# A selective-scan network: sums of product pairs on GpSimd, PSUM banks of two pools in turn, and the last stage in reversed column order

## Chip, cores, metric

The kernel runs on one core of one Trainium2 chip. The metric is the device time of one execution in microseconds. The times before are the median of three runs; the profile comes from one profiled execution of its own.

## What is computed

The input x has the shape (8, 64, 64, 64): eight images of 64 channels, 64 x 64 pixels, in float32. Four layers follow one another:

```
x = layer0(x)   # attention over all 4096 pixels, then 3x3 depthwise, 1x1, and x is added
x = layer1(x)   # layer norm; two blocks of 8x8 window attention and an MLP (the second shifted)
x = layer2(x)   # nine taps with dynamic filters, leaky relu, a 9-tap row convolution, plus x
x = layer3(x)   # selective scan in four directions, gating, then pooled depthwise branches
```

The part that the change touches most is the scan of layer 3. For each image, direction k, channel (128 of them) and state n (16 of them), over the 4096 pixels in the order of the direction:

```
h = h * exp(dt_t[..., None] * A) + dt_t[..., None] * B_t[:, :, None, :] * u_t[..., None]
y_t = einsum('bkcn,bkn->bkc', h, C_t)
```

The four directions' y are summed, normalised over the channels, gated with silu(z), and projected. The rest of layer 3 (`back` below) adds that to its input, normalises over the channels again, and forms four depthwise branches, three of them after max pooling by 2, 4 and 8, which are aggregated, passed through gelu, multiplied and added.

## The kernel before, in words

Images are handled in four pairs; the 128 partitions are two images of 64 channels, or the 128 channels of one image's scan. A pair has three parts, in class `_Direct`:

- `front(p)` (line 1225): layer 0 to layer 2, then `scan_sources` (line 1549), which leaves the scan's inputs and the gate z in DRAM.
- `scans(p, ...)` (line 1614): 64 units (2 images x 4 directions x 8 blocks of 512 columns), each of 8 steps of two states: 512 steps.
- `back(p)` (line 1748): what follows the scan. A first loop over 8 blocks of 512 columns (lines 1754 to 1774) reads ys of both images, normalises, gates, projects and adds, and normalises over the channels into the padded tile F. The pooled branches follow (1777 to 1802), then a second loop over the 8 blocks (1803 to 1826), with the depthwise taps of the full-size branch and the output.

`tile_kernel` (line 1831) runs front(0) alone, then for each pair p the scans with back(p-1) and front(p+1) beside them, and at the end back(3) alone. `front` and `back` are generators that yield costs. `scans` draws from them so that their summed cost keeps pace with the steps: `while done < cost * (i + 1) / (n - LEAD)`, with LEAD = 24, so the work beside should be out of the way 24 steps before the end. The cost of a back is put at a quarter of a front's; by its own yields it comes to 264 units against 2,016, so that it runs out earlier: in phases 1 and 2 some 67 steps before the end, in the last phase, which has back(2) alone beside it, at about the middle. After that `next(beside, cost)` returns the whole cost.

A step (`step`, line 1682) handles states n and n+1. Two steps ahead, GpSimd has formed v = B * du for both (1680, 128 x 1024). ScalarE writes da = exp(A dt) into a PSUM bank (1700), VectorE scans (1703), ScalarE copies the last column into the carries (1711). Then the products with C: `rp` is `i % 2 or u["image"] >= B - 2` (1689). Where it is 0 (even steps of images 0 to 5), GpSimd does both states in one instruction of 1024 columns (1714). Where it is set, GpSimd does one state (1716) and VectorE the other (1717). One step later `sums` (1719) adds the two products to y with two matmuls against the identity (1730); each matmul shows as two records in the profile. After eight steps y goes to Y or, for the last direction, to ys in DRAM (1739 to 1745). The directions run in the order 1, 3, 0, 2; direction 2 goes through the column blocks from 7 down to 0.

Each fetch of B and C (1675, 512 KB each) is issued on SP's queue, as are the scan's inputs (1652, 1668), ys (1745) and the loads of back (1756, 1761, 1762).

[...] Pool `ps_scan` holds three of tag "da" (da, and pdd and pbc of `inputs`, 1654 and 1663) and one for y; pool `ps_front` holds three of tag "f", which `bank()` (1178) gives to front and back, and one for `total()`. The order of instructions on each engine isn't the program's: the framework's scheduler arranges it when the kernel is built, with program order as the priority.

Of the kernel before, what the change touches and what calls it, by code (L numbers as in the profile page):

```python
# [9 lines left out]
F32 = mybir.dt.float32  # L10
AF = mybir.ActivationFunctionType
ALU = mybir.AluOpType
# [3 lines left out]
B, C, HH, WW = 8, 64, 64, 64  # L16
L = HH * WW
P = 128
CH = 512
NCH = L // CH  # L20
# [3 lines left out]
DI, NST, RNK, KDIR = 128, 16, 4, 4  # L24
TD = 512
# [1122 lines left out]
class _Direct:  # L1148
# [8 lines left out]
    def __init__(self, net, ctx):  # L1157
        self.net, self.tc, self.nc, self.w = net, net.tc, net.nc, net.w
        tc = self.tc
        self.dram = ctx.enter_context(tc.tile_pool(name="mem", bufs=2, space=bass.MemoryType.DRAM))  # L1160
        one = ctx.enter_context(tc.tile_pool(name="scan1", bufs=1))
        self.Y = one.tile([P, L], F32, name="Y", tag="Y")
        self.carries = one.tile([P, NST], F32, name="carry", tag="carry")
        self.sw = ctx.enter_context(tc.tile_pool(name="scan", bufs=2))
        self.slabs = ctx.enter_context(tc.tile_pool(name="slabs", bufs=3))
        self.ps = ctx.enter_context(tc.tile_pool(name="ps_scan", bufs=3, space=PSUM))
        self.pf = ctx.enter_context(tc.tile_pool(name="ps_front", bufs=3, space=PSUM))
        self.kept = {}

    def padded(self, name):  # L1170
        t = self.slabs.tile([P, SLAB], F32, name=name, tag="slab").rearrange("p (h w) -> p h w", w=66)
# [3 lines left out]
    def flat(self, name):  # L1175
        return self.slabs.tile([P, SLAB], F32, name=name, tag="slab")[:, 0:L]

    def bank(self, name, shape=(P, CH)):
        return self.pf.tile(list(shape), F32, name=name, tag="f")

    def total(self, name, shape=(P, CH)):
        return self.pf.tile(list(shape), F32, name=name, tag="acc", bufs=1)
# [431 lines left out]
    def scans(self, p, beside, cost):  # L1614

        self.units = []
        for im in range(2):
            out = self.memory("ys")  # L1620
            self.kept["y", 2 * p + im] = out
            for nth, k in enumerate((1, 3, 0, 2)):
                order = range(NTD) if k < 2 else range(NTD - 1, -1, -1)
                self.units += [dict(image=2 * p + im, k=k, c=c, at=at, nth=nth, out=out) for at, c in enumerate(order)]
        self.inputs(self.units[0])
        n = 8 * len(self.units)
        steps = [{} for _ in range(n)]
        done = 0
        for i in range(-3, n):
            if i + 3 < n:  # L1630
                self.fetch(i + 3, steps[i + 3], 0)
            if 0 <= i + 2 < n:
                self.fetch(i + 2, steps[i + 2], 1)
                self.products(i + 2, steps[i + 2])
            if i >= 0:
                self.step(i, steps[i])
                if i:
                    self.sums(i - 1, steps[i - 1], steps[i]["w"])
                while done < cost * (i + 1) / (n - LEAD):
                    done += next(beside, cost)  # L1640
            if i % 8 == 1 and i // 8 + 1 < len(self.units):
                self.inputs(self.units[i // 8 + 1])
        self.sums(n - 1, steps[n - 1])
        self.run(beside)
# [37 lines left out]
    def step(self, i, st):  # L1682

        nc, w, net = self.nc, self.w, self.net
        wk, ps = self.sw, self.ps
        u = self.units[i // 8]
        k, c, at, CC, v = u["k"], u["c"], u["at"], st["C"], st["v"]

        n0, rp = 2 * (i % 8), i % 2 or u["image"] >= B - 2
        rev = k >= 2  # L1690

        def along(t):
            return t[:, ::-1] if rev else t

        h = wk.tile([P, 2 - i % 2, TD], F32, name="hd", tag=f"h{i % 2}", bufs=1)
        hs = []
        for j in range(2):
            n = n0 + j
            da = ps.tile([P, TD], F32, name="dad", tag="da")
            nc.scalar.activation(da, u["du"][:, 0], AF.Exp, scale=net.As[:, k, n : n + 1])  # L1700
            first = 0.0 if at == 0 else self.carries[:, n : n + 1]
            to = da if rp and j else h[:, j]
            nc.vector.tensor_tensor_scan(along(to), along(da), along(v[:, j]), first, ALU.mult, ALU.add)  # L1703
            hs.append(to)
            if at < NTD - 1 and (rp or j):
                ends = h[:, :, 0] if rev else h[:, :, TD - 1]
                cs = self.carries[:, n0 : n0 + 2]
                if rp:
                    ends = to[:, 0:1] if rev else to[:, TD - 1 : TD]
                    cs = self.carries[:, n : n + 1]  # L1710
                nc.scalar.activation(cs, ends, AF.Copy)  # L1711

        if rp == 0:
            st["w"] = nc.gpsimd.tensor_tensor(v, h, CC, ALU.mult)  # L1714
        else:
            st["w"] = nc.gpsimd.tensor_tensor(v[:, 0], h[:, 0], CC[:, 0], ALU.mult)  # L1716
            nc.vector.tensor_tensor(v[:, 1], hs[1], CC[:, 1], ALU.mult)  # L1717

    def sums(self, i, st, after=None):

        nc, w, net = self.nc, self.w, self.net
        wk, ps = self.sw, self.ps
        u = self.units[i // 8]
        k, c = u["k"], u["c"]
        if i % 8 == 0:
            u["y"] = ps.tile([P, TD], F32, name="yd", tag="y", bufs=1)
        y = u["y"]
        for j in range(2):
            n = 2 * (i % 8) + j
            m = nc.tensor.matmul(y, lhsT=w["ident"], rhs=st["v"][:, j], start=(n == 0), stop=(n == NST - 1))  # L1730
            if after is not None and j == 0:
                net.behind(m, after)
        if i % 8 < 7:
            return

        yd = net.part(self.Y, k, c)
        yp = y.rearrange("p (a b) -> p a b", b=64)
        if u["nth"] == 0:
            nc.vector.scalar_tensor_tensor(yd, self.img(u["x"]), net.dsum, yp, ALU.mult, ALU.add)
        elif u["nth"] < 3:  # L1740
            nc.vector.tensor_tensor(yd, yd, yp, ALU.add)  # L1741
        else:
            o = wk.tile([P, TD], F32, name="yo", tag="yo", bufs=1)
            nc.vector.tensor_tensor(self.img(o), yd, yp, ALU.add)
            nc.sync.dma_start(u["out"][:, c * TD : (c + 1) * TD], o)


    def back(self, p):
        nc, tc, w, net, half = self.nc, self.tc, self.w, self.net, self.HALF
# [1 line left out]
        X = self.flat("X3")  # L1751
        F = self.padded("F")
        with tc.tile_pool(name="w4", bufs=2) as wk:
            for c in range(NCH):
                cols = slice(c * CH, (c + 1) * CH)
                nc.sync.dma_start(X[:, cols], self.kept["x", p][:, cols])
                po = self.bank("po3")
                for im in range(2):
                    y = wk.tile([P, CH], F32, name="yb", tag="yb")
                    z = wk.tile([P, CH], F32, name="zb", tag="zb")  # L1760
                    nc.sync.dma_start(y, self.kept["y", 2 * p + im][:, cols])
                    nc.sync.dma_start(z, self.kept[2 * p + im][2][:, cols])
                    pc, sd = self.normed(wk, lambda pc: [(pc, y)], w["cen128"], w["avg128"], net.eps[:, 0:1])
                    u = wk.tile([P, CH], F32, name="u", tag="u")
                    nc.vector.scalar_tensor_tensor(u, pc, w["on_g"], sd, ALU.mult, ALU.mult)  # L1765
                    nc.vector.scalar_tensor_tensor(u, u, w["on_b"], z, ALU.add, ALU.mult)  # L1766
                    nc.tensor.matmul(po[half[im]], lhsT=w["opT"], rhs=u, start=True, stop=True)  # L1767
                    yield 6
                nc.vector.scalar_tensor_tensor(X[:, cols], po, w["outproj_b"], X[:, cols], ALU.add, ALU.add)  # L1769
                pc, sd = self.normed(wk, lambda pc: [(pc, X[:, cols])], w["cen64"], w["avg64"], net.eps[:, 1:2])  # L1770
                d = self.rows(F, c)
                nc.vector.scalar_tensor_tensor(d, self.img(pc), w["cn_g"], self.img(sd), ALU.mult, ALU.mult)
                nc.scalar.activation(d, d, AF.Identity, bias=w["cn_b"])
                yield 6
# [56 lines left out]
def tile_kernel(ctx: ExitStack, tc: tile.TileContext, x: bass.AP, packs, layout, out: bass.AP):  # L1831
    net = _Net(ctx, tc, x, packs, layout, out)
    with ExitStack() as path:
        net.open(path, True)
        d = _Direct(net, path)
        net.log_exp()
        front = d.run(d.front(0))
        back = 0.25 * front
        for p in range(B // 2):
            works, cost = [], 0  # L1840
            if p:
                works.append(d.back(p - 1))
                cost += back
            if p + 1 < B // 2:
                works.append(d.front(p + 1))
                cost += front
            d.scans(p, d.chain(*works), cost)
        d.run(d.back(B // 2 - 1))
# [31 lines left out]
```

## Time and profile before

| | us |
|---|---|
| median of 3 runs | 14083.28 (14071.26 to 14084.42) |
| profiled execution, its own time | 14074.21 |
| its span in the profile | 14072.3 |
| PE busy | 11340.1 (81%) |
| VectorE (DVE) busy | 8432.1 (60%) |
| ScalarE (ACT) busy | 7036.3 (50%) |
| GpSimd (POOL) busy | 8173.2 (58%) |
| mean granted PE clock | 0.865 |

The profile lists the busy time of each engine, the span in 40 slices of 352 us, and the costliest groups of instructions by line: how many, how long in all and each, and how long the engine sat idle just before them and for whom. Times are counted from the start of the span. A PE record's end is modelled, since matmuls are pipelined, so start-to-start distances say more than durations there. PEld are weight loads, which overlap with matmuls.

### The profile page before, as it was taken

Reading aid. Unit: us, or ns where it says so; the run is one execution under the profiler, and the core shown is the slowest. Engines: PE = TensorE matmul, PEld = TensorE weight load, DVE = VectorE, ACT = ScalarE, POOL = GpSimd, SP = SyncE. Lnnn points to the kernel's source line nnn. Section 1 sums busy time; section 2 is a strip of 40 time slices with the busy share of each in tenths; the row PEclk is TensorE's granted clock in tenths of the full one; section 3 lists DMA queues with packets and bytes.
Section 4 is the critical chain, followed back from the end, with each engine's and each line's share of the span. In section 5 each row is a group of like instructions: output and inputs, shape, how many; then the busy total and the mean of one; then the engine's idle time right before and its main releaser. Section 6 shows DMA issues by size and latency. Waiting matters only on the chain. (4 is left out here: it accounts for less than half of the span.)

```text
span 14072.3 us, 141532 instructions
## 1 busy us (share of the span) xinstructions
PE 11340.1 (81%) x46358; PEld 4189.8 (30%) x46358; DVE 8432.1 (60%) x9763; ACT 7036.3 (50%) x15453; POOL 8173.2 (58%) x4111
## 2 busy tenths in 40 slices
PE   9888879979889668998889666998988866666665
PEld 2244222224433222223433222222443222222221
DVE  0222254467776875347675767336666677998884
ACT  5533145555553645555562644555554454454442
POOL 0000035677776765456674685456666678879991
PEclk9866679989889889998898788999888878988996
DMA  0000034456555764345553675345554577878882
GB/s 17 1 1 1 5 136 153 161 187 211 195 196 181 241 206 156 127 147 181 175 197 133 225 247 180 128 144 175 170 173 168 181 244 256 276 241 291 294 291 70
DMA packets 705498, 2379.22 MB, mean 169 GB/s; under 512 B 81060, under 2 KB 81188, under 8 KB 703980
## 3 DMA queue, kind: packets, MB, share of 16 engines
q1 hardware_dynamic: 681024, 2315.57, 48.5%
q10 hardware_dynamic: 23724, 54.50, 1.0%
q8 instruction: 367, 6.01, 0.2%
q14 instruction: 383, 3.14, 0.1%
HBM read 2269.08 MB, written 100.66 MB: 168 GB/s over the span
## 5 line engine op out<-in xcount | busy, mean ns | idle before, releaser
L1680 POOL TENSOR_TENSOR vd<-B,du 128x1024 f32<-128x1024 f32 x2048 | 4842.5, 2369 | 3955.8 <-DVE xacc L1217 1888.8
L1730 PE MATMUL yd<-vd,pack 128*128 128x512 f32 x8192 | 4577.0, 686 | 1175.1 <-POOL vd L1714 419.8
L1703 DVE TENSOR_TENSOR_SCAN hd<-dad,carry,vd 128x512 f32<-128x512 f32 x2464 | 3092.6, 1270 | 1081.7 <-ACT dad L1700 681.2
L1700 ACT ACTIVATE dad<-du,As 128x512 f32<-128x512 f32 x4096 | 2711.7, 679 | 985.0 <-DVE hd L1703 728.8
L1730 PEld LDWEIGHTS yd<-vd,pack 128*128 128x128 f32 x8192 | 1592.5, 212 | 3853.7 <-issue 1753.0
L1714 POOL TENSOR_TENSOR vd<-hd,C 128x1024 f32<-128x1024 f32 x768 | 1810.9, 2358 | 1365.4 <-DVE hd L1703 694.1
L1716 POOL TENSOR_TENSOR vd<-hd,C 128x512 f32<-128x512 f32 x1280 | 1634.9, 1278 | 271.7 <-DVE hd L1703 244.6
L1272 ACT ACTIVATE e<-s 128x512 f32<-128x512 f32 x2048 | 1199.2, 591 | 1030.0 <-PE s L1266 1028.1
L1703 DVE TENSOR_TENSOR_SCAN dad<-dad,carry,vd 128x512 f32<-128x512 f32 x1120 | 1426.0, 1273 | 62.7 <-ACT dad L1700 62.5
L1266 PE MATMUL s<-X 64*128 64x512 f32 x4096 | 1350.1, 646 | 114.1 <-ACT e L1272 113.8
L1258 PE MATMUL po<-e,VT 128*64 128x512 f32 x4096 | 1145.1, 629 | 17.0 <-ACT e L1272 17.0
L1711 ACT ACTIVATE carry<-hd 128x1 f32<-128x1 f32 (+1 forms) x1792 | 357.1, 201 | 1172.7 <-DVE hd L1703 1161.9
L1717 DVE TENSOR_TENSOR vd<-dad,C 128x512 f32<-128x512 f32 x1280 | 858.7, 671 | 82.1 <-ACT carry L1711 74.8
L1266 PEld LDWEIGHTS s<-X 64*128 64x128 f32 x4096 | 365.3, 186 | 1065.4 <-issue 820.8
L1420 PEld LDWEIGHTS w_av<-vals,w_e 64*64 64x64 f32 x16384 | 612.7, 159 | 178.0 <-ACT w_e L1410 69.9
L1420 PE MATMUL w_av<-vals,w_e 64*64 64x9 f32 x16384 | 638.5, 216 | 23.6 <-ACT w_e L1410 23.5
L1703 DVE TENSOR_TENSOR_SCAN hd<-dad,vd 128x512 f32<-128x512 f32 x352 | 420.2, 1210 | 203.0 <-ACT dad L1700 92.0
L1741 DVE TENSOR_TENSOR Y<-Y,yd 128x512 f32<-128x512 f32 x128 | 124.6, 973 | 656.0 <-PE yd L1730 655.7
L1410 ACT ACTIVATE w_e<-w_e 128x512 f32<-128x512 f32 x512 | 310.4, 627 | 382.2 <-DVE w_e L1405 254.9
L1655 PE MATMUL pdd<-xs,xdt 128*128 128x512 f32 x512 | 323.4, 718 | 204.3 <-DVE hd L1703 96.7
L1711 ACT ACTIVATE carry<-dad 128x1 f32<-128x1 f32 x1120 | 189.9, 170 | 589.1 <-DVE dad L1703 587.0
L1405 DVE TENSOR_TENSOR w_e<-w_s,bias 128x512 f32<-128x512 f32 x512 | 328.5, 682 | 248.4 <-PE w_s L1393 248.1
(247 smaller groups left out, 11078.1 us busy)
## 6 DMA issues: line engine op xcount, KB each, us to landing
B<-rows SPq DMA_DIRECT2D x2048, 512.0 KB, 5.0
C<-rows SPq DMA_DIRECT2D x2048, 512.0 KB, 4.5
xs<-xt SPq DMA_DIRECT2D x128, 256.0 KB, 2.9
xs<-xc SPq DMA_DIRECT2D x128, 256.0 KB, 3.1
xc<-xcv ACTq DMA_DIRECT2D x64, 256.0 KB, 4.3
zs<-z ACTq DMA_DIRECT2D x64, 256.0 KB, 3.9
xt<-XT ACTq DMA_DIRECT2D x32, 512.0 KB, 7.5
rows<-bc SPq DMA_DIRECT2D x256, 64.0 KB, 1.9
```

Of the source, the lines that this page charges most:

```text
L1258: nc.tensor.matmul(po[half[im]], lhsT=VT[:, t, half[im]], rhs=es[im], start=(t == 0), stop=(t == 31))
L1266: nc.tensor.matmul(ss[im], lhsT=at(half[im], t), rhs=X[half[im], jc * CH : (jc + 1) * CH], start=True, stop=True)
L1272: nc.scalar.activation(e, ss[im], AF.Exp, scale=C**-0.5, accum_out=parts[:, im, t, jc : jc + 1])
L1420: nc.tensor.matmul(self.av[half[im], x % 4 + j, h, :], lhsT=es[h // 4][half[im], j, h % 4, :], rhs=V[half[im], x + j, h, :], start=True, s ...
L1680: self.nc.gpsimd.tensor_tensor(v, st["B"], dx.to_broadcast([P, 2, TD]), ALU.mult)
L1700: nc.scalar.activation(da, u["du"][:, 0], AF.Exp, scale=net.As[:, k, n : n + 1])
L1703: nc.vector.tensor_tensor_scan(along(to), along(da), along(v[:, j]), first, ALU.mult, ALU.add)
L1711: nc.scalar.activation(cs, ends, AF.Copy)
L1714: st["w"] = nc.gpsimd.tensor_tensor(v, h, CC, ALU.mult)
L1716: st["w"] = nc.gpsimd.tensor_tensor(v[:, 0], h[:, 0], CC[:, 0], ALU.mult)
L1717: nc.vector.tensor_tensor(v[:, 1], hs[1], CC[:, 1], ALU.mult)
L1730: m = nc.tensor.matmul(y, lhsT=w["ident"], rhs=st["v"][:, j], start=(n == 0), stop=(n == NST - 1))
```

## The change

Four edits. `bank()` gets a second tag and a counter `turn`: while it is not negative, successive tiles are taken in turn from tag "f" of one pool and tag "da" of the other, so from six banks in place of three. It is not negative while front(0) runs alone, and in the last phase from the moment when the work beside is exhausted, to the end of the kernel; `da` of a step is then drawn in the same way. On even steps of images 0 to 5 GpSimd adds the second product to the first after it has formed both, and `sums` issues one matmul for that step in place of two. And the first loop of `back` goes through the column blocks from 7 to 0, in every pair.

```diff
@@ __init__
         self.kept = {}
+        self.turn = -1
@@ bank
-    def bank(self, name, shape=(P, CH)):
-        return self.pf.tile(list(shape), F32, name=name, tag="f")
+    def bank(self, name, shape=(P, CH), ours="f"):
+        if self.turn >= 0:
+            self.turn += 1
+            ours = ("f", "da")[self.turn % 2]
+        return (self.pf if ours == "f" else self.ps).tile(list(shape), F32, name=name, tag=ours)
@@ scans
                     self.sums(i - 1, steps[i - 1], steps[i]["w"])
+                if p == B // 2 - 1 and done >= cost:
+                    self.turn = max(self.turn, 0)
@@ step
-            da = ps.tile([P, TD], F32, name="dad", tag="da")
+            da = self.bank("dad", (P, TD), "da")
@@ step
         if rp == 0:
-            st["w"] = nc.gpsimd.tensor_tensor(v, h, CC, ALU.mult)
+            nc.gpsimd.tensor_tensor(v, h, CC, ALU.mult)
+            st["w"] = nc.gpsimd.tensor_tensor(v[:, 0], v[:, 0], v[:, 1], ALU.add)
+            st["n"] = 1
@@ sums
-        for j in range(2):
-            n = 2 * (i % 8) + j
-            m = nc.tensor.matmul(y, lhsT=w["ident"], rhs=st["v"][:, j], start=(n == 0), stop=(n == NST - 1))
+        n = st.get("n", 2)
+        for j in range(n):
+            m = nc.tensor.matmul(
+                y, lhsT=w["ident"], rhs=st["v"][:, j], start=(i % 8 + j == 0), stop=(i % 8 == 7 and j == n - 1)
+            )
@@ back, first loop
-            for c in range(NCH):
+            for c in reversed(range(NCH)):
@@ tile_kernel
+        d.turn = 0
         front = d.run(d.front(0))
+        d.turn = -1
```

## The prediction

> **What bounds the kernel now.** I read the page first, then one table of busy times cut at the stages of the work that runs beside the scans (I found the cuts from the first and last instruction of each stage's lines), then the costliest groups, the waits inside a stage, and the timeline of the two stretches where one side runs alone.
>
> ```profile
> span 14072.3 us, 141532 instructions
> ...
> PE 9888879979889668998889666998988866666665
> ...
> POOL 0000035677776765456674685456666678879991
> ...
> PEclk9866679989889889998898788999888878988996
> ```
> Three regimes. GpSimd (POOL) does nothing for the first 1,890 us: the front of pair 0 runs alone. Then come three scan phases beside other work (POOL's first product of each: 1905, 4990, 8348 us), a fourth from 11700 us that ends at 13785 us, and 287 us of the last back alone.
>
> The stage table, columns: stretch, length, busy us (and count) of PE, PE weight loads, DVE, ACT, POOL, then clock and DMA.
> ```profile
> 2003.00:2955.00 952.00, 911.31 (x2664) 251.82 (x2664) 412.17 (x388) 554.97 (x1567) 570.91 (x278) 0.98 0.48 162
> ...
> 3136.00:4130.00 994.00, 881.17 (x7042) 424.96 (x7041) 726.04 (x888) 600.01 (x1154) 755.69 (x368) 0.90 0.60 204
> ...
> 6285.00:6447.00 162.00, 105.36 (x278) 42.13 (x277) 153.76 (x175) 68.84 (x135) 132.48 (x64) 0.81 0.59 208
> 6450.00:7352.00 902.00, 804.81 (x6869) 396.00 (x6867) 610.94 (x786) 537.08 (x1015) 598.57 (x291) 0.89 0.53 180
> 7355.00:7742.00 387.00, 356.94 (x718) 130.34 (x718) 212.08 (x254) 113.18 (x235) 197.68 (x96) 0.88 0.41 138
> ...
> 8029.00:8348.00 319.00, 198.94 (x336) 66.25 (x334) 211.39 (x198) 139.16 (x285) 280.72 (x139) 0.85 0.72 251
> ...
> 12640.00:13785.00 1145.00, 755.09 (x1354) 244.90 (x1353) 955.67 (x981) 538.53 (x1298) 1054.98 (x596) 0.90 0.84 288
> ```
> In order: attention of layer 0 (PE 96% of phase 0's stretch), windows with their MLPs (PE 89%), depthwise (DVE 95%), windows of phase 1, layer 2 (PE 92%), the tail where the scan runs alone (POOL 88%), and the scan-only half of phase 3 (POOL 92%). So the limit changes from stage to stage: PE in attention, windows, layer 2; DVE in depthwise; POOL in the tails. One average says nothing.
>
> ```profile
> L1680 POOL TENSOR_TENSOR vd<-B,du 128x1024 f32<-128x1024 f32 x2048 | 4842.5, 2369 | 3955.8 <-DVE xacc L1217 1888.8
> L1730 PE MATMUL yd<-vd,pack 128*128 128x512 f32 x8192 | 4577.0, 686 | 1175.1 <-POOL vd L1714 419.8
> ...
> L1714 POOL TENSOR_TENSOR vd<-hd,C 128x1024 f32<-128x1024 f32 x768 | 1810.9, 2358 | 1365.4 <-DVE hd L1703 694.1
> ...
> L1716 POOL TENSOR_TENSOR vd<-hd,C 128x512 f32<-128x512 f32 x1280 | 1634.9, 1278 | 271.7 <-DVE hd L1703 244.6
> ```
> 8192 records for 4096 sum matmuls: two records each. A record's 686 ns is modelled to its end; from start to next start in attention of phase 1 it is 0.507 us (215 us for 424 records), so one matmul occupies PE 1.01 us.
>
> ```profile
> POOL vd L1680 <- PE yd L1730: 259.9, 56, 8.2
> ```
> In that stage POOL itself waits 260 of 896 us for PE to free the product buffers: PE is late, POOL early.
>
> **What the Trainium skill says.** "GPSIMD Engine Reference", section 3.1, puts a two-input elementwise operation at about 2.6 cycles per element; at its 1.2 GHz that is, as an estimate, 1.11 us for 512 columns, and the trace has 1.278 us for exactly this shape (L1716): it agrees once some overhead is added, and the trace's figure is used. "TensorE: Matmul & The Clock Gate", Part 1, says that PE runs at half clock until it has been kept busy; the trace agrees: records start 0.43 us apart when dense and 0.85 us in the last back, where the clock row shows 0.54. "SBUF — State Buffer", section "SBUF: two separate sides", says that DVE and GpSimd block each other where the DVE instruction has two SBUF inputs. The scans and products (L1703, L1717) have one, the other is in PSUM; in the trace L1703 takes 1.264 us wholly under a POOL instruction and 1.266 us under none, so I charge nothing for more POOL work.
>
> **The change, part by part.**
> *The add.* In phases 0 to 2 the even steps (L1714, x768) get one more POOL instruction of 512 columns and lose one of four sum matmuls per pair of steps. Added: 768 x 1.278 = 981 us of POOL. Removed: 768 x 1.01 = 776 us of PE. The add depends on the product just ahead of it; no dependent pair on POOL is in the trace. Back-to-back POOL instructions overlap by 0.05 us, so the lower bound is 1.23 us; for the upper I allow 1.5 us (a handover of about 0.2 us, as seen between ACT and DVE). I take 1.28. Queued behind it on POOL: the next B product and the next C product, for which the scan and the sums wait. A pair of steps then needs 2 x 2.369 + 2.358 + 2 x 1.278 = 9.65 us of POOL, 4.83 per step, where it was 4.19.
> - Attention: 548 + 436 + 436 records; a quarter less at 0.507 us is 180 us. POOL has room (0.51 to 0.60). I take 170 off; bounds 130 to 185.
> - Windows: 740 + 583 + 584 records, a quarter is 477, 243 us of PE. PE is idle 11% for its own chain, so not all counts. Steps take 5.40 us in phase 0 (184 steps), 6.18 in phases 1 and 2 (146 each). At a POOL share of 0.90 a step cannot go below 5.37, so phase 0 gives some 15 and the others 45 each: 105 off; bounds 30 to 190.
> - Layer 2: 628 records, a quarter at 0.507 is 80; PE 92%: 60 off; bounds 30 to 80.
> - Depthwise: 99 steps at 5.1 us; POOL goes from 0.82 to 0.95 and joins DVE: 20 on. Scan sources (152 steps; POOL 0.76 in phase 0): 10 on.
> - Tails: POOL is the bound. From 4.73 to 5.37 us per step over 134 steps is 83, and 12 for the 20 steps of phase 0: 95 on. Bounds of these three lines together 60 to 200.
> Phase 3 has no even-step product of 1024 columns and is untouched. Sum: -170 -105 -60 +20 +10 +95 = **-210 us**.
>
> *The banks.* The order on each engine is not the program's order (L1312 of a chunk sits in the middle of the next chunk's depthwise taps), so it is chosen ahead, and a tile seems to get its bank in the order of first use within its tag. Evidence: in the last back the im 1 centring matmul (13839.43 us) goes only after po3's first write (13837.53), though a bank was free from 13833.2; and y of column block 1 is not fetched at 12843 us though its slot is free, because y of block 0, image 7, stands before it. With two tags in turn, a tile waits only for every second predecessor. The MLP alone:
> ```profile
> 1010.74 1.13 PE L1485 MATMUL ph<-m_h,pack 64*128 64x512 f32 x4 [2.32 <-DVE m_h L1481]
> 1012.61 2.55 PE L1492 MATMUL pf<-hid,pack 128*64 128x512 f32 x4 [0.74 <-ACT hid L1487]
> 1015.09 1.66 PE L1201 MATMUL pc<-X,pack 128*128 128x512 f32 x2
> ```
> pc of the next chunk stands behind pf; it may now go behind ph, and its 2.4 us (1015.09 to the next start, 1017.43) leave the chain: 16 chunks, 38 us. The window heads are alike (pc 769.04 to pv 771.85, behind w_ot): 16 rows x 1.6 to 2.8, about 35. In the scan sources DVE idles from 1870 to 1900 us since pz runs on one free bank, 2.85 us each: about 20. Attention (PE 540.00 of 540 us) and the depthwise taps (DVE) gain nothing. 90 off. Against it, the first pdd (1886 us, overlapping the front's last 70 us) now stands behind the front's tiles of its own tag: 10 on, since only two steps had been done by 1960. **-80 us**; bounds 0 to 150. In phase 3 dad takes both tags once back(2) is exhausted: POOL is at 0.92 there, so at most a few us.
>
> *Columns from the last on.* The last units of a phase (k = 2) write ys from column block 7 down to 0. Before, back's first block needs the last one written, so everything behind it waits for the phase's end. Reversed, in the tails of phases 0 to 2 block after block can be done early, in slack of DVE (0.66) and PE (0.62). Moved ahead of the next phase: 36 us of DVE (8 x 6 x 0.75), some 64 matmuls, and on SP's queue the loads of X, y and z, each y behind its store, among the fetches of B and C. That helps where DVE bounds (0.81 early in phases 1 to 3): **-45 us**; bounds +20 (fetches delayed) to -100. At the very end the dads hold both tags to the end, so PE work cannot move ahead; only the loads do. Saved: the wait 13785.8 to 13790.5 and a little, 8 us, plus per block the overlap of the second image's pc and square, about 2 us x 8; phase 3's end gives the rest: **-30 us**; bounds -10 to -60.
>
> Sum: -210 -80 -45 -30 = -365. The profiled execution took 14074.2 us (span 14072.3); the median, 14083.3, is 9 us more. **Forecast 13,709 us, say 13,710.**
>
> **Rivals.**
> (a) *POOL saturates earlier.* If it can't pass 0.83, its share in depthwise, a step costs at least 5.82 us: windows +77 -90, depthwise +72, scan sources +26, tails +146, against -230 from attention and layer 2: +1. With -130 from the rest: 13,945. For: yd waits for L1714 and L1716 already; against: 0.92 in phase 3.
> (b) *Slower.* The add sits between product and sum, and POOL, strictly in order, passes its delay to the next B product; if dependences cap POOL at 0.79, a step takes 6.11 us: windows +131 -20, depthwise +102, sources +44, tails +185, against -230: +212; banks and order then bring 50: 14,236. It decides below a share of about 0.81. Against: products run two steps ahead with six buffers.
> (c) *The order brings more.* Blocks done in the tails and the warm clock of a denser PE at both ends: front -150, reversal -100, end -60, windows -150: 13,540.
> (d) *The ordering of banks is as before*, and only the add acts: 13,864.
>
> **How the numbers follow.** Forecast 0.48, (a) 0.20, (b) 0.07, (c) 0.15, (d) 0.10. The range goes from (c) to (a). About 0.2% is what a measurement here can tell from no change. Faster takes all cases but (b), less 0.03 for the upper end of (a): 0.90; same 0.03; slower 0.07.
>
> **What would show it.** Right: attention at 6.3 and 7.6 us per step with PE still near 0.95; 768 more POOL records of 512 columns at 1.28 us and 6656 sum records; tails near 5.4 us per step; pc behind ph in the MLP; back's matmuls inside the tails. Wrong: PE share in windows falling as much as its work, with waits of yd for the added instruction, or POOL below 0.85 in the tails.

## The result, and the profile after

The changed kernel takes 14269.31 us (median of 4 runs, 14264.85 to 14289.0) against 14077.27 us for the kernel before (median of 4 on the same chip): a ratio of 1.014, 95% interval 1.0123 to 1.0158. It is slower by 1.4%, where 13,710 us, a gain of 2.6%, was forecast; the forecast's range ended at 13,945 us.

From the page of the changed kernel:

```profile
span 14267.3 us, 139329 instructions
...
POOL 0000056688877876677676796658666788878882
PEclk9866779978888679998788677998788868888887
```

GpSimd works more nearly everywhere (9125.8 us busy, from 8173.2), PE less (11078.2 us, from 11340.1), and its mean granted clock is 0.826, from 0.865. GpSimd now starts in slice 6 at 5 tenths where it had 3: the front that runs alone is over sooner, and the attention of the next pair starts at 1904 us, 100 us earlier.

The stages, cut at the first and last instructions of the same lines as before (columns: stretch, length, busy us and count of PE, PE weight loads, DVE, ACT, POOL, then clock, DMA share and GB/s):

```profile
1904.00:2888.00 984.00, 907.80 (x2546) 239.56 (x2544) 427.56 (x403) 559.50 (x1588) 684.15 (x362) 0.93 0.49 162
3072.00:4135.00 1063.00, 872.93 (x6860) 419.82 (x6862) 739.12 (x895) 607.91 (x1166) 882.33 (x467) 0.83 0.58 194
6299.00:6477.00 178.00, 106.19 (x277) 40.92 (x277) 165.78 (x192) 77.68 (x154) 167.02 (x87) 0.78 0.63 215
6477.00:7426.00 949.00, 793.80 (x6724) 396.20 (x6722) 612.93 (x784) 536.03 (x1012) 691.65 (x367) 0.82 0.51 171
7426.00:7796.00 370.00, 332.67 (x658) 119.74 (x656) 202.28 (x243) 110.15 (x223) 210.24 (x111) 0.87 0.40 136
8089.00:8439.00 350.00, 202.65 (x274) 60.72 (x272) 211.86 (x202) 142.08 (x292) 324.13 (x173) 0.68 0.66 227
12774.00:14014.00 1240.00, 801.20 (x1384) 275.95 (x1383) 987.32 (x1009) 562.74 (x1337) 1083.81 (x611) 0.85 0.80 273
```

The windows of phases 0 and 1 before, with the same cut:

```profile
3127.00:4128.00 1001.00, 883.69 (x7045) 425.76 (x7043) 733.50 (x891) 603.71 (x1160) 760.27 (x370) 0.90 0.60 204
...
6445.00:7349.00 904.00, 806.92 (x6875) 397.47 (x6874) 612.28 (x786) 537.62 (x1017) 603.57 (x293) 0.89 0.53 180
```

Attention of phase 0 is 984 us, not 952; windows of phase 0 are 1063, not 1001; windows of phase 1 are 949, not 904, with PE busy for only 794 of them (84%, was 89%) and POOL for 692 (73%, was 67%); layer 2 is shorter, 370 for 387; the tail is 350 for 319. The second half of phase 3, which has no added instruction at all, is 1240 us for 1162, cut where back(2) ends; over the same last 304 steps it is 64 us longer. No engine is at its limit in the windows of phase 1, and yet they are 45 us longer, with PE busy for 13 us less.

The sums and the added instruction, which the forecast priced:

```profile
L1739 PE MATMUL yd<-vd,pack 128*128 128x512 f32 x6656 | 4047.6, 733 | 1604.5 <-POOL vd L1722 755.8
...
L1722 POOL TENSOR_TENSOR vd<-vd 128x512 f32<-128x512 f32 x768 | 980.7, 1277 | 35.0
```

The counts and the price of the instruction came as forecast: 768 adds of 1277 ns, 981 us, and 6656 sum records. The 35 us of idle time before the adds belong to the 447 of them that stand directly behind their own product: these start 0.078 us after its end, where independent GpSimd neighbours overlap by 0.042 us (medians of this trace). A dependent pair thus costs 0.12 us more, some 54 us in all. What is new stands at the end of the L1739 row: PE sits idle before its sums for 1604 us, 1175 before, and the largest part, 756 us, ends with the *added* instruction (before: 420 us with the product).

By kind of stage, in us against the profiled run of before, summed over the phases. The columns after the first two are experiments told below; each is cut in its own trace. The profiled execution of the add alone is 40 us above the median of that kernel, so its column sums to more than its median shows. Sums of a stage that an edit could hardly reach moved by up to 20 us (the windows, where only the last phase was changed), so differences of that size say little.

| stages | forecast | after | add alone | add, both matmuls kept | one matmul left out, no add | sums later, no add | add, sums later |
|---|---|---|---|---|---|---|---|
| front(0) alone | -90 (+10 after it) | -100 | -8 | -13 | -7 | -14 | -15 |
| attention | -170 | -28 | -40 | +128 | -58 | -15 | +113 |
| depthwise | +20 | +46 | +46 | +17 | +5 | +51 | +5 |
| windows | -105 | +153 | +149 | +145 | -33 | +43 | +78 |
| layer 2 | -60 | -27 | -17 | +30 | -77 | +64 | +12 |
| scan sources | +10 | +20 | +23 | +25 | +7 | +5 | +19 |
| tails | +95 | +73 | +68 | +90 | +10 | +22 | +70 |
| starts of phases 1, 2 (back) | most of -45 | +25 | +30 | +17 | +4 | 0 | +54 |
| phase 3, second half | a few | +78 | +11 | -4 | -10 | +30 | +31 |
| after the last scan | -30 | -34 | -2 | 0 | 0 | 0 | -2 |

The first half of phase 3 is 10 us shorter in the changed kernel, and up to 22 us longer in these runs. The forecast misses by some 560 us: 258 of them in the windows, 142 in attention, 68 in phase 3 as a whole, some 70 where the reversed order was to help and the starts of phases got longer.

### The profile page after: what moved, and what is told of

It reads as the page before. It is cut to its first block, busy times and chain, and to the rows that moved or that the text cites. A ratio compares the mean times of both kernels' runs of the same rounds, so it can differ in the third digit from the quotient of the medians.

```text
span 14267.3 us, 139329 instructions
## 1 busy us (share of the span) xinstructions
PE 11078.2 (78%) x44822; PEld 4068.7 (29%) x44822; DVE 8420.7 (59%) x9763; ACT 7034.3 (49%) x15461; POOL 9125.8 (64%) x4879
## 5 line engine op out<-in xcount | busy, mean ns | idle before, releaser
L1739 PE MATMUL yd<-vd,pack 128*128 128x512 f32 x6656 | 4047.6, 733 | 1604.5 <-POOL vd L1722 755.8
L1739 PEld LDWEIGHTS yd<-vd,pack 128*128 128x128 f32 x6656 | 1349.6, 224 | 4018.6 <-issue 1443.8
L1263 PE MATMUL po<-e,VT 128*64 128x512 f32 x4096 | 1207.4, 639 | 32.7 <-ACT e L1277 32.7
L1722 POOL TENSOR_TENSOR vd<-vd 128x512 f32<-128x512 f32 x768 | 980.7, 1277 | 35.0
L1425 PEld LDWEIGHTS w_av<-vals,w_e 64*64 64x64 f32 x16384 | 662.7, 170 | 210.8 <-ACT w_e L1415 89.2
L1425 PE MATMUL w_av<-vals,w_e 64*64 64x9 f32 x16384 | 690.8, 222 | 29.1 <-ACT w_e L1415 28.1
```

The costliest lines, as they stand in the source:

```text
L1263: nc.tensor.matmul(po[half[im]], lhsT=VT[:, t, half[im]], rhs=es[im], start=(t == 0), stop=(t == 31))
L1425: nc.tensor.matmul(self.av[half[im], x % 4 + j, h, :], lhsT=es[h // 4][half[im], j, h % 4, :], rhs=V[half[im], x + j, h, :], start=True, s ...
L1722: st["w"] = nc.gpsimd.tensor_tensor(v[:, 0], v[:, 0], v[:, 1], ALU.add)
```

## The experiments

Theory 1: the added instruction's time counts on the path, though GpSimd has idle time in every stage, since it lies in the chain of a step (product, scan, product with C, add, sum) and each engine takes its instructions in a fixed order. Theory 2: fewer matmuls let PE's granted clock fall (0.89 to 0.82 in the windows), and the slower PE makes the stages longer. The first four runs take the change apart.

**The add alone**: the diff of `step` and `sums`, nothing else.

> Only the add on GpSimd and the dropped matmul of even steps; banks and column order as before. If the add is what lost the time (as the stages of the changed kernel suggest: windows 902 to 938 us, depthwise 162 to 191, tails 319 to 350), this alone is 170 to 280 us slower than before (14,250 to 14,360). The prediction's own step says 210 us faster.

Measured: 14303.01 us, ratio 1.0159 (1.0137 to 1.0181), 235 us more. The add alone is more than the whole loss of 192; the other edits together bring a little.

**Both tags for front(0) alone**: `d.turn = 0` before `d.run(d.front(0))`, `d.turn = -1` behind it.

> Only the two tags in turn while front(0) runs alone. Both theories: 80 to 110 us faster, all of it before the second front's attention begins; the scan phases keep their lengths within 15 us each.

Measured: 13996.99 us, ratio 0.9948 (0.9929 to 0.9966), 71 to 77 us less. The stage itself is 100 us shorter, and about 20 come back in the attention that follows, which starts with fewer products with B done (4 against 10). The forecast's -90 and +10 are right in kind and nearly in size. So is the mechanism: in 15 of 16 chunks of the MLP pc now stands behind ph, where it stood behind pf, and a chunk takes about 8.3 us in place of 11.8.

**da in turn in the last phase alone**: the two lines in `scans` and the draw of `da` from `bank`.

> Only the two tags in turn from the middle of the last phase to the end. If the turn of da rearranges GpSimd's order in the scan-only half of phase 3, that half goes from 1160 to about 1240 us and the kernel is 40 to 80 us slower, with the last back 15 to 35 us shorter. If that half's loss comes from elsewhere, the kernel is 15 to 40 us faster. The prediction's step said a few us gained there.

Measured: 14118.51 us, ratio 1.0034 (1.0025 to 1.0043): slower. The second half of phase 3 is 69 us longer, the end 32 shorter.

**Reversed order of back alone**: `for c in reversed(range(NCH))`.

> Only the reversed first loop of back. The prediction's step: 45 us faster in the phases, and since the last back's tiles are not held up by da here, its blocks can be done before the scan ends: up to 150 us more at the end. If fetches and in-order engines are disturbed instead: 0 to 30 us slower in the phases.

Measured: 14004.27 us, ratio 0.9950 (0.9935 to 0.9964). But the gain is not where it was forecast: the starts of the phases gain 14 us, not 45, and what follows the last scan falls from 287 to 236 us. In that kernel the last back's tiles have tag "f" to themselves, and 9 of the 32 records of its projections (po) come before the last sum, 2 before the change; in the whole change `da` holds both tags there, as the prediction said, none does, and the end gains only 34.

**The add without its saving.** Both matmuls stay, and the sum goes into the used-up C tile, where nobody reads it.

```diff
-            st["w"] = nc.gpsimd.tensor_tensor(v[:, 0], v[:, 0], v[:, 1], ALU.add)
-            st["n"] = 1
+            nc.gpsimd.tensor_tensor(CC[:, 0], v[:, 0], v[:, 1], ALU.add)
```

> GpSimd adds the two products of even steps as in the change, but into the used-up C tile, where nobody reads it; both sum matmuls stay as before. Theory 1 (the add's time in GpSimd's queue delays what stands behind it): 200 to 350 us slower than before, windows 100 to 200 us longer over the three phases. Theory 2 (what hurts is that PE, with fewer matmuls, falls to a lower clock): 0 to 100 us slower, windows within 60 us, PE clock in windows near 0.89.

Measured: 14525.31 us, ratio 1.0311 (1.0293 to 1.0329): +438 us for 981 us of GpSimd. No sum needs this add, and still attention gets 40 to 47 us longer in each phase, where POOL is busy for 0.56 of the time (0.66 in phase 0). The C tile, which the add holds longer, is not what costs: GpSimd waits 13 us for loads of C in all, 37 before.

**The saving without the add.** The second product of the even steps of images 0 to 5 is left out of y: one matmul, no add.

> Even steps issue only the first of their two sum matmuls and nobody adds: the second product of each even step of images 0 to 5 is left out of y. Theory 1: 150 to 335 us faster (the prediction's own figure for the removed matmuls is 335). Theory 2: between 50 us faster and 100 us slower, with PE's clock in windows near 0.82 as in the changed kernel.

Measured: 13908.95 us, ratio 0.9867 (0.9848 to 0.9886): -178 us, where the forecast counted -335 for the three stages. Together the two runs give +260, close to the +235 of the add alone. So two terms failed: the added work costs 438 and not some 125 (the forecast's 20, 10 and 95), and the removed work brings 178 and not 335. How the two share the sum depends on these two kernels, in which the add writes elsewhere or isn't there. Stage by stage the two runs do not add up so well: in attention +128 and -58 stand against -40 for the add alone, in the depthwise stage +17 and +5 against +46. The order on the engines is built anew for each kernel, so a stage's number belongs to the kernel it was measured in.

**PE kept busy.** The add, and in place of the removed matmul one with a matrix of zeros, which adds nothing to y.

```diff
+        if n == 1:
+            nc.tensor.matmul(y, lhsT=self.zero, rhs=u["du"][:, 0], start=False, stop=False)
```

> The add alone (as e1), with a second matmul per even step that adds zero (zero weights, an operand long ready), so that PE has as many matmuls as before and only the wait for the add is new. Theory 1: as slow as e1 or slower, 14,300 to 14,450. Theory 2: faster than e1, 14,050 to 14,200, windows within 50 us of before.

Measured: 14582.79 us, ratio 1.035 (1.0331 to 1.0369): 280 us above the add alone, and above what either theory expected. The clock in the windows of phase 1 is back at 0.89, and the stage is 949 us long, as with the add alone (948); the windows of all three phases are 183 us longer than before, where the add alone made them 149. For the windows Theory 2 has fallen: with the clock given back they are no shorter. For attention no run decides. With both matmuls kept the clock there fell from 0.97 to 0.94 in phase 1, and PE, which is close to its limit, was busy for 31 us more with as many matmuls (882 for 851); how much of the 47 us is the clock stays open.

**A mix**: both tags in front(0), reversed back, `da` with its own tag, and the add only while attention of phases 1 and 2 or layer 2 runs beside (a flag set by `front`).

> A version put together from what e1 to e4 showed: banks in turn in front(0), reversed back, no turn of da in the last phase, and the add only in steps beside attention of phases 1 and 2 and beside layer 2. Sum of the parts: -71 -64 -60 (attention) -20 (layer 2) = about 215 us faster than before, 13,850. If the add's gain in a stage is given back in the next (same steps, later), about 140 us faster, 13,930.

Measured: 13858.05 us, ratio 0.9832 (0.9813 to 0.9851). Faster than both kernels, and as the sum of the parts had it (13,850).

**The add in another place in GpSimd's queue**: issued in the next step, behind that step's product with B.

```diff
+            if i >= 1 and steps[i - 1].get("n", 2) == 1:
+                v = steps[i - 1]["v"]
+                self.nc.gpsimd.tensor_tensor(v[:, 0], v[:, 0], v[:, 1], ALU.add)
             if i >= 0:
                 self.step(i, steps[i])
```

> The add alone, as in the run of the add alone, but GpSimd adds in the next step, behind that step's product with B and ahead of its product with C. The add's work is the same 981 us; only its place in GpSimd's queue moves. Theory 1a (what costs is the place: the next product with B, and the scan that takes it, stand behind the add): about half of what the add costs in the queue comes back, 14,050 to 14,150 us, and the windows of phases 1 to 3 lose clearly less than the 149 us of the add alone. Theory 1b (what costs is GpSimd's time itself, in whatever place, since the product with C of the odd step still waits for it): 14,260 to 14,330, within 0.3% of the add alone, windows again near +150.

Measured: 14398.15 us, ratio 1.0231 (1.021 to 1.0252). Both expectations missed: it is slower still, by some 95 us. So the next B product behind the add can't be all that costs: with that product ahead of the add, and the add later, the kernel is worse. That turned the question to what waits for the add itself.

**Tags and order without the add** (front(0), reversed back, own tag for `da`), **the mix with fewer adds** (none beside layer 2 in phase 0; those beside attention and layer 2 in phases 1 and 2 stay), and **that mix with the late add**:

> The front that runs alone takes both tags, the back goes from the last columns on, da keeps its tag in the last phase, and there is no add. If the parts are independent: the before time less 71 (both tags in front 0) less 64 (reversed back), 13,935 to 13,950 us. If they share a gain (both would have to act on the same stage, which the stage tables don't show): 13,980 to 14,000.

> As the mixed kernel, with the add beside layer 2 of phases 1 and 2 alone, and not of phase 0, where it cost 21 us. If what the add does to a stage holds stage by stage: 13,858 less 21, about 13,835 us. If the gain of the add in attention and layer 2 is given back at the next stage: no change, 13,850 to 13,865.

> As the kernel with fewer adds, with each add behind the next step's product with B. Theory 1a: the add beside attention and layer 2 costs less on the scan's side, so 20 to 50 us faster than the same kernel with the add in its first place. Theory 1b: within 10 us of it.

Measured: 13938.63 us, ratio 0.9904 (0.9886 to 0.9923); 13833.81 us, ratio 0.9832 (0.9812 to 0.9852), the lowest median of the study; 13947.99 us, ratio 0.991 (0.9888 to 0.9931). The first two fit the sums of parts, 13,935 to 13,950 and 13,835. The two mixes ran on different chips and have the same ratio to the kernel before, so that fewer adds are better is not shown. The adds that are left are worth 105 us (13938.63 without any). The third contradicts both theories' numbers again: with the late add the 42 us that attention gains become a loss of 28.

**Sums a step later.** In the windows of phase 1, the view of the sum's tile lists until when its engine sat idle before it (us, times). The kernel before, then the changed one:

```profile
its engine sat idle before it (us, times) until:
...
  POOL vd L1714: 57.1, 36
...
who waited for it (us, times):
...
  PEld ph L1485: 14.1, 5
```

```profile
its engine sat idle before it (us, times) until:
  POOL vd L1722: 120.4, 55
...
who waited for it (us, times):
...
  PEld ph L1490: 31.1, 9
```

These 120 us add up weight loads and matmuls, which wait for the same instruction at the same time:

```profile
PEld yd L1739 <- POOL vd L1722: 74.3, 31, 6.1
...
PE yd L1739 <- POOL vd L1722: 46.0, 24, 5.3
```

Counted once, the sum stands 74 us at the head of PE's queue for the added instruction, where it stood 37 for the product before: 37 us more, in a stage that got 45 longer, and matmuls of the window work (ph) wait behind, 31 us for 14. In the run with one matmul left out the same place reads:

```profile
  POOL vd L1719: 111.3, 56
```

Here PE has less to do, comes to the sum earlier, and waits there: the removed matmul turns in part into a wait (57 to 111 us in this view, 37 to 67 counted once). Theory 3: beside the windows the cost is this wait. So the sums are ordered two steps back, where the add has long been done (one more call behind the loop is not shown):

```diff
-                if i:
-                    self.sums(i - 1, steps[i - 1], steps[i]["w"])
+                if i > 1:
+                    self.sums(i - 2, steps[i - 2], steps[i]["w"])
```

> The add alone, but the sums in PSUM of a step are ordered two steps back and not one, so that they meet an added instruction that has long been done. Theory 3 (what the add costs beside the attentions is TensorE standing at the sum, in its own queue, for the added instruction): the waits of yd for the add in the windows of phase 1, 75 us of weight load and 49 of matmul with the add alone, fall below those of the kernel before, 37 and 20; the windows of phases 1 and 2 come back by 40 us or more each, and the whole to 14,060 to 14,170 us. Theory 1 (GpSimd's own queue: the products behind the add come late, whenever the sums are taken): 14,270 to 14,340, windows within 15 us of the add alone. The sums hold their tile of products a step longer, which could cost either by itself: see the run of the later sums alone.

> The kernel before with its sums two steps back and no add. Theory 3: the waits of yd for the product with C (37 and 20 us in these windows) fall, so a gain of 0 to 60 us, 14,010 to 14,080. Against it: the tile of products is held a step longer, GpSimd waits for the sums to free it (104 us in these windows already), a loss of up to 100 us, 14,080 to 14,180.

> The kernel with the add beside attention and layer 2 of phases 1 and 2, with the sums two steps back. Theory 3: the same kernel less what the later sums bring in the run without an add, and some 10 to 30 us more; 13,750 to 13,830. Theory 1: 13,830 to 13,860, and above that by what the later sums cost alone.

Measured: 14467.2 us, ratio 1.0281 (1.0258 to 1.0304); without an add 14288.08 us, ratio 1.0155 (1.0133 to 1.0176); the mix with fewer adds 14169.88 us, ratio 1.0063 (1.0042 to 1.0085). In the windows of the first:

```profile
  POOL vd L1721: 19.4, 13
```

The wait is all but gone, and with it most of the add's cost in the windows: 78 less 43 is 35 us in the three phases, where it was 149. There Theory 3 holds in kind, though the windows of phases 1 and 2 came back by some 25 us each and not by the 40 expected. The sum needn't wait for the add itself: in the run with both matmuls kept, where nothing needs the add, the windows lost as much (145 us), and PE's waits at the sums for GpSimd's products grew from 69 to 116 us in phase 1 (weight loads and matmuls added up). A late GpSimd result at the head of PE's queue is what the two have in common.

But the whole does not get better. The later sums alone cost 220 us, more than the 100 allowed for, though they take away nearly half of PE's idle time before the sums (1175 us before):

```profile
L1736 PE MATMUL yd<-vd,pack 128*128 128x512 f32 x8192 | 4399.9, 671 | 627.5 <-POOL vd L1722 253.2
```

On top of them the add still costs 179, most of it now in attention (+113 against -15). So this wait is not *the* cause: take it away in one place and the lateness comes out in another. That a later sum holds its tile of products a step longer may be why it costs by itself; no run shows it.

**The add on VectorE**, with the later sums:

```diff
+                if i and steps[i - 1].get("n", 2) == 1:
+                    v = steps[i - 1]["v"]
+                    self.nc.vector.tensor_tensor(v[:, 0], v[:, 0], v[:, 1], ALU.add)
```

> As the add with the later sums, but VectorE adds, in the next step behind its scans, so GpSimd's work is that of the kernel before. The scan's chain gets an addition of some 0.67 us in every second step on VectorE, 515 us over 768 steps, of which beside the attentions little lies on the path. Theory 1 (GpSimd's time): the loss in the windows is gone and the removed matmuls show, as in the run without them: 13,900 to 14,050. Theory 3 alone, with GpSimd's time free: no better than the add on GpSimd with later sums, within 40 us of it.

Measured: 14803.76 us, ratio 1.0514 (1.0491 to 1.0537), the slowest. Both expectations missed, for a reason of its own, and the run says nothing on the theories:

```profile
L1644 DVE TENSOR_TENSOR vd<-vd 128x512 f32<-128x512 f32 x768 | 1469.9, 1914 | 498.5 <-POOL vd L1723 496.0
```

An addition put at 0.67 us takes 1.914 us. Of the 768, the 75 with no GpSimd product under them take 0.683 us each, the other 693 take 2.047. The Trainium skill's "SBUF — State Buffer", section "SBUF: two separate sides", which the prediction cited for the scans, names just this case, two SBUF inputs on VectorE; here the trace agrees.

**Two last runs**: the whole change without `da`'s turn in the last phase, and the mix with fewer adds with both tags for the last back.

> The whole change without the one place where da takes turns in the last phase; the front that runs alone keeps both tags, the back goes from the last columns on, GpSimd adds in every second step. If the parts add up as measured alone: 14,070 plus 235 less 71 less 64, about 14,170 us, and the stretch behind the last scan near 236 us as with the reversed order alone. If the turn of da in the last phase costs nothing in the whole change: 14,250 to 14,280.

> The kernel with the add beside attention and layer 2 of phases 1 and 2, and both tags for the last back, which runs behind the scans, while da keeps its tag. If the blocks of the last back wait for banks: 10 to 30 us less than the same kernel without it, 13,800 to 13,825. If a bank of tag da comes free only behind the last exps of the scan, so that its first blocks start late: 13,835 to 13,860.

Measured: 14187.48 us, ratio 1.0078 (1.0056 to 1.0099), against 14,170 from the sum of the parts; and 13854.69 us, ratio 0.9841 (0.9824 to 0.9859), with an end of 255 us against 237 for the same mix without. So the turn costs 82 us inside the whole change, and both tags are no help to the last back. Of the 82, 61 lie in the second half of phase 3 and 19 at the end. The waits of that half (VectorE, then GpSimd; us, times, longest), first in the changed kernel:

```profile
DVE hd L1710 <- POOL vd L1687: 115.9, 130, 3.2
DVE dad L1710 <- POOL vd L1687: 91.3, 76, 3.0
...
POOL vd L1687 <- DMA B<-rows: 53.1, 47, 2.6
POOL vd L1725 <- issue: 51.1, 20, 2.6
POOL vd L1725 <- DMA C<-rows: 23.1, 16, 1.7
```

Without the turn:

```profile
DVE hd L1708 <- POOL vd L1685: 46.0, 96, 0.9
...
POOL vd L1723 <- DVE hd L1708: 46.1, 41, 3.3
POOL vd L1685 <- DMA B<-rows: 40.7, 31, 2.8
POOL vd L1723 <- DMA C<-rows: 2.6, 3, 1.3
```

GpSimd, the busiest engine there, idles 152 us with the turn and 93 without. Its timeline in one stretch (start, us, then idle time before it in brackets), first with the turn:

```profile
13322.22 1.27 POOL L1725 TENSOR_TENSOR vd<-hd,C 128x512 f32<-128x512 f32 x1 [2.62 <-issue]
13323.45 4.66 POOL L1687 TENSOR_TENSOR vd<-B,du 128x1024 f32<-128x1024 f32 x2
13328.06 2.49 POOL L1725 TENSOR_TENSOR vd<-hd,C 128x512 f32<-128x512 f32 x2
```

```profile
13317.37 2.36 POOL L1685 TENSOR_TENSOR vd<-B,du 128x1024 f32<-128x1024 f32 x1
13319.68 1.26 POOL L1723 TENSOR_TENSOR vd<-hd,C 128x512 f32<-128x512 f32 x1
13320.90 2.36 POOL L1685 TENSOR_TENSOR vd<-B,du 128x1024 f32<-128x1024 f32 x1
```

In this stretch products with B and C alternate without a gap where there is no turn; with it they come in pairs, a scan waits for the second of two B products, and GpSimd for the scan. Both kernels have stretches of both kinds; over the last 304 steps two B products follow each other 63 times with the turn and 51 without. A step takes 4.08 us (1240 us by 304 steps) in place of 3.88. The queue's contents are the same; the order in it, made when the kernel is built, is another.

## Why the prediction was wrong, point by point

*The add, attention.* The step that failed: "POOL has room (0.51 to 0.60). I take 170 off". It put the add at nothing there and nearly all of the removed PE work at its full time. Room is a share of time; the add's 1.28 us lies in the chain of a step. Measured, attention gained 28 us and not 170. The run of the add with both matmuls kept shows the path. Attention of phase 1 before, and in that run (engine, who waits for whom: us, times, longest):

```profile
PEld s L1266 <- ACT e L1272: 74.7, 45, 4.3
...
ACT carry L1711 <- DVE hd L1703: 65.8, 78, 4.7
```

```profile
PEld s L1271 <- ACT e L1277: 96.0, 53, 5.6
...
ACT carry L1716 <- DVE hd L1708: 85.0, 73, 5.9
```

Scans come later, ScalarE stands longer at a carry or a `da`, attention's exponentials stand behind these in its queue, and PE waits for them: 21 us more in the rows shown (its matmuls wait at the same times as its weight loads), of the 47 by which the stage got longer. The other 26 are not accounted for; the lower clock, told above, may be in them. The Trainium skill's "Perfetto Trace Analysis", section "Tensor Engine Instruction (MATMUL, LD_WEIGHTS)", says that ScalarE, VectorE and GpSimd take their instructions strictly in order, and that PE can do little more than draw weight loads ahead; the waits above fit. With the removed matmuls (some 52 us of PE in this stage, from start to start) the changed kernel keeps 30 us in phases 1 and 2, and in phase 0 nothing (+33). The removal alone brings only 16 and 20 us of these 52: the forecast took nearly all of PE's work for time. That PE, done earlier, waits for others in place of it is the likely reason.

*The add, windows.* "105 off" became +153. The step that failed is the price of the add: it entered only as a floor, "At a POOL share of 0.90 a step cannot go below 5.37", which steps of 6.18 us don't touch, so that it cost nothing in phases 1 and 2 and 45 us each were taken off for PE's work. No share bounds these windows; a late add or product at the head of PE's queue costs there (37 us waited in phase 1 before, 74 after), with POOL at 0.73. The number of steps in the stage hardly moves between kernels (147 in both; 148 with the matmul left out), since the order on every engine is fixed when the kernel is built; so, as I read it, a late step can't be caught up elsewhere, and the stage takes its 147 steps at 6.45 us each where it was 6.16. Of the 243 us of PE work removed here the forecast counted 105 as time; leaving out the matmuls alone brings 33.

*Layer 2, depthwise, sources, tails*: -27 for -60, +46 for +20, +20 for +10, +73 for +95. Kinds right; the tail's step at 5.3 us (350 us by 66) came as forecast, 5.37.

*The price of the add* was right: 1.277 us for 1.28. So was the doubt about a dependent pair: the handover costs 0.12 us where add follows product directly, below the 0.2 allowed for.

*The banks.* Front(0): right in mechanism and size, 71 to 77 us for 80. Phase 3: "so at most a few us" failed; +69 with the turn alone, and 61 inside the whole change. It weighed GpSimd's share and overlooked that drawing `da` from two tags gives the scheduler another order to build. That it does so is shown; why pairs of B products come of it is not.

*Columns from the last on*: of -45 in the phases, 14 came when tried alone: the term was too large, and why the early blocks save no more isn't shown. The end was priced rightly for the whole change (-34 for -30); without the turn it is -53.

*The rivals.* (b), the slower one, came nearest: 14,236 us, given 0.07. That is luck in part, for its mechanism, a cap on POOL's share at 0.79, isn't what happened: POOL reaches 0.93 in the tails and 0.94 in depthwise, and in the windows, at 0.73, it is far below the cap. What the prediction named under "Wrong", a falling PE share with waits of yd for the added instruction, is what the trace shows. A slip in (c): its four parts and the forecast's other terms make 13,509 us, not 13,540.

*Left open*: why the add costs about as much in all (179 us on top of the later sums, 235 without) when its wait in the windows is gone; the later sums change the built order and the life of the product tiles at once, and no run separates these. Whether a longer ring of product tiles would help wasn't tried.

## What to carry to other kernels

An engine with idle time isn't free for an instruction that is put into the chain between two others: ask who stands at the head of which in-order queue waiting for its result, and what other work is behind. Work taken from such a queue is worth only what doesn't become a wait at the next result. And a wait that a view lists isn't yet time: later sums nearly halved PE's idle time before the sums and made the kernel slower. Try an edit stage by stage: here the same add gains 30 us in attention of phase 1 and loses 45 in the windows behind it, and kept only where it gains, it makes the kernel with the other two gains faster (13833.81 us, 13938.63 without an add).

## What the hardware showed that was not expected

- VectorE's addition of two SBUF tiles of 512 columns takes 0.683 us alone and 2.047 us with GpSimd's products under it, and 318 of 2048 GpSimd products of 1024 columns took over 2.6 us in that kernel (43 in the kernel before), where 2.35 is the median.
- PE's granted clock went with its busy share in the windows of phase 1: 0.89 at a share of 89%, 0.82 at 84%. With matmuls of zeros in place of those removed it is back at 0.89, and the stage is no shorter (949 and 948 us).
- An add directly behind the GpSimd product that it needs starts 0.078 us after that product's end (447 cases); independent neighbours overlap by 0.042 us.
